# A sparse attention kernel: each query's first edge without TensorE, and gathers that skip empty places by a bound on the row number

## The chip, the cores and the metric

One core of one Trainium2 chip. The time is the device time of one launch in microseconds (us), the median of several executions. In the experiments the kernel before ran beside the others on the same chip; a ratio is the mean time of one kernel's fast runs over that of the kernel before in the same rounds, so it is not quite the ratio of the medians quoted.

Engine names in the profile: PE is TensorE, DVE is VectorE, ACT is ScalarE, POOL is GpSimd, SP is SyncE (it issues plain DMAs). "Granted clock" is the share of full speed that the throttle left to TensorE.

## The reference, cut to what matters

Graph attention on 16 batches of 1024 nodes, 512 wide, 8 heads, one adjacency matrix for all batches, then a residual and a normalisation:

```python
q = (x @ Wq + bq);  k = (x @ Wk + bk);  v = (x @ Wv + bv)       # heads of 64
scores = einsum('bqhd,bkhd->bhqk', q, k) / sqrt(64) + (1 - adj) * -1e9
out = einsum('bhqk,bkhd->bqhd', softmax(scores), v) @ Wo + bo
return layernorm(x + out)
```

The adjacency has 4043 edges of a million places, so the kernel works edge by edge. A query without an edge (60 of them) gets the mean of all rows of v; this is why a batch's gathers cannot start before its mean row exists. All four biases are zero in these inputs; one experiment uses that.

## The kernel before

A batch has eight tiles of 128 queries. A tile's edges are laid out in blocks of 128 places; a block is gathered as one row of q and one row of k|v for each place. VectorE makes the products and scores, ScalarE the exponentials, VectorE weighs v with them (`pv`), and TensorE adds the places of each query with a 0/1 matrix (`sums`). Then come the division, a transposition (`poT`), the product with Wo (`po`), the residual and the normalisation. GpSimd adds the output bias to a tile's residual rows `y` ahead of the residual, and raises the variance to the power -1/2 (`rstd`, the "root" of the prediction). y_1, y_5 are the second and the sixth of these additions at a change of batch, counted from y_0.

The order of instructions is fixed by one loop over blocks. In each step it issues a gather some blocks ahead, the VectorE work of the next blocks, the sum of this block, and then spends a credit of TensorE time on large products: `finishing` (po of tiles done) or, if there is none, `fronts` (q, k, v of the next batch).

```python
BLOCKS = (11, 6, 4, 4, 3, 3, 3, 3)           # blocks of the eight tiles: 37 per batch

def load_y(b, t):                            # the residual rows of a tile
    Y[b, t] = work.tile([P, D], F32, tag="y", bufs=7)
    nc.sync.dma_start(Y[b, t], x[b, ds(t * P, P), :])
    later(2, lambda: nc.gpsimd.tensor_tensor(Y[b, t], Y[b, t], bo_bc, op=OP.add))

def gather(n):
    ...
    nc.gpsimd.indirect_dma_start(out=QG[n], in_=q_rows[b % 2], ...)    # 128 rows of q
    nc.gpsimd.indirect_dma_start(out=KG[n], in_=kv_rows[b % 2], ...)   # 128 rows of k|v

def add_up(n):
    if i == 0:
        SUM[b, t] = psum.tile([P, 2, HALF], F32, tag="sum", bufs=2)
    nc.tensor.matmul(SUM[b, t][:, 0, 0:HD2], m, pv[:, 0:HD2], **kw)
    nc.tensor.matmul(SUM[b, t][:, 1, 0:HD2 + HEADS], m, pv[:, HD2:], **kw)

while ...:                                   # one step per block n
    if front_batches < B and front_batches <= max(n // NB, 0) + 1:
        fronts += ...                        # the next batch's products become available
    elif n % NB == 0:
        share = (sum(u[0] for u in fronts) + tiles * NPAIR * PRODUCT) / NB
    ... gather(gathered); weigh(n + 1); scores(n + 2)
    for fn in plan.pop(n, ()): fn()          # what `later` has put here
    ... exponentials(n + 2); add_up(n)
    for tile_done in done[:2]:
        if tile_done not in Y: load_y(*tile_done)
    ... spend the credit on finishing or fronts
```

## Time and profile before

| | before |
|---|---|
| time, median | 2593.45 us (2592.3 to 2593.49) |
| TensorE busy | 96% |
| granted clock, mean | 0.982 |
| period of one batch (mean of 13) | 153.7 us |
| TensorE idle at a change of batch | 1.9 us |

From the page of the kernel before, the 40 slices of TensorE, GpSimd and the granted clock (a digit is tenths busy, or tenths of full clock):

```profile
PE   6988999999999999999999999999999999999967
POOL 0156755647566574756647465564756557475675
PEclk9989999999999999999999999999999999999978
```

TensorE is full except at both ends. GpSimd looks half idle, which says nothing about whether it is late at one moment of each batch. Its gathers, as groups (busy us and mean ns of one, idle time before them and what ended most of it):

```profile
L506 POOL DMA_INDIRECT kvg<-kv_rows,key_row x592 | 588.7, 994 | 195.2 <-issue 182.9 <-DMA kv_rows<-mean 7.8 <-ACT pv L522 1.7
L501 POOL DMA_INDIRECT qg<-q_rows,query_row x592 | 586.9, 991 | 588.1 <-DVE s L517 453.7 <-issue 81.3 <-DVE stats L471 30.4
```

A pair of gathers costs GpSimd two microseconds, 592 times. And the waits of TensorE between 430 and 2420 us, that is without the two end batches (total, times, longest):

```profile
PE sum L545 <- DVE pv L533: 26.8, 15, 1.9
PE poT L566 <- DVE o L557: 1.8, 10, 0.2
```

### The profile page before, as it was taken

How to read it: one execution, taken by the hardware profiler on the slowest of the kernel's cores; microseconds unless marked ns; L12 is line 12 of the kernel's file. 1: busy time of each engine (PE TensorE's matmuls, PEld its weight loads, DVE VectorE, ACT ScalarE, POOL GpSimd, SP SyncE). 2: the span in 40 equal slices, each digit the busy share in tenths (PEclk: the TensorE clock that was granted, in tenths of full speed). 3: DMA queues.
4: the chain of work that ended last, by engine and by line, in shares of the span. 5: the costliest groups of instructions: out<-in, count | busy, mean ns of one | idle time of the engine just before them, and what ended most of it. 6: DMA issues, size and time to landing. Idle time of an engine off the chain costs nothing.

```text
span 2594.1 us, 26742 instructions
## 1 busy us (share of the span) xinstructions
PE 2477.6 (96%) x7659; PEld 1352.6 (52%) x7659; DVE 1968.2 (76%) x3613; ACT 698.7 (27%) x1764; POOL 1499.0 (58%) x1717
## 2 busy tenths in 40 slices
PE   6988999999999999999999999999999999999967
PEld 3545555555555555555555555555555555555534
DVE  5668778778778877877777777877877777787766
ACT  1345322222222222222222222222222222222254
POOL 0156755647566574756647465564756557475675
PEclk9989999999999999999999999999999999999978
DMA  4368887887879788787878878787887978878785
GB/s 154 110 243 290 270 291 247 286 270 271 283 237 307 254 291 267 257 292 244 301 253 292 271 235 306 244 294 256 277 288 233 309 251 287 264 256 287 230 277 179
DMA packets 228679, 678.01 MB, mean 261 GB/s; under 512 B 29454, under 2 KB 29466, under 8 KB 228524
## 3 DMA queue, kind: packets, MB, share of 16 engines
q0 software_dynamic: 132608, 465.64, 56.3%
q1 hardware_dynamic: 93344, 205.60, 21.2%
q10 hardware_dynamic: 2572, 4.99, 0.5%
q8 instruction: 62, 1.02, 0.2%
q14 instruction: 93, 0.76, 0.1%
HBM read 541.86 MB, written 134.25 MB: 261 GB/s over the span
## 4 chain that ended last, share of the span: by engine, by line
PE 68%; POOL 11%; DVE 10%; issue 7%; ACT 2%; DMA 1%; ACTq 0%; POOLq 0%; another core or an unknown queue 0%; SPq 0%; DVEq 0%
PE pv L377 16%; PE pk L377 15%; PE pq L377 15%; PE sum L546 7%; PE sum L545 7%; POOL kvg L506 4%; PE po L377 4%; POOL y L461 3%; POOL qg L501 2%; DVE y L468 2%; DVE stats L471 2%; PE pxT L359 2%; PE poT L566 2%; DVE qg L515 1%; DVE pv L533 1%
## 5 line engine op out<-in xcount | busy, mean ns | idle before, releaser
L501 POOL DMA_INDIRECT qg<-q_rows,query_row x592 | 586.9, 991 | 588.1 <-DVE s L517 453.7
L506 POOL DMA_INDIRECT kvg<-kv_rows,key_row x592 | 588.7, 994 | 195.2 <-issue 182.9
L533 DVE TENSOR_TENSOR pv<-kvg,pv 128x512 f32<-128x512 f32 x550 | 394.3, 717 | 223.1 <-ACT pv L522 146.8
L377 PE MATMUL pq<-wq,xT 128*128 128x512 f32 x1024 | 482.7, 597 | 14.7 <-ACT xT L363 13.2
L377 PE MATMUL pk<-wk,xT 128*128 128x512 f32 x1024 | 488.9, 598 | 7.1 <-ACT xT L363 7.1
L377 PE MATMUL pv<-wv,xT 128*128 128x512 f32 x1024 | 479.1, 593 | 0.0
L377 PE MATMUL po<-wo,oT 128*128 128x512 f32 x1024 | 473.9, 602 | 0.0
L515 DVE TENSOR_TENSOR qg<-qg,kvg 128x512 f32<-128x512 f32 x592 | 432.6, 731 | 0.3 <-issue 0.3
L517 DVE TENSOR_REDUCE s<-qg 128x8 f32<-128x512 f32 x592 | 406.1, 686 | 20.5
L545 PE MATMUL sum<-pv,sums 128*128 128x256 f32 x1184 | 361.6, 387 | 46.4 <-DVE pv L533 33.8
L545 PEld LDWEIGHTS sum<-pv,sums 128*128 128x128 f32 x1184 | 222.2, 192 | 326.5 <-issue 239.0
L522 ACT ACTIVATE pv<-s 128x8 f32<-128x8 f32 x592 | 124.1, 210 | 929.2 <-DVE s L517 626.5
L546 PE MATMUL sum<-pv,sums 128*128 128x264 f32 x1184 | 366.6, 392 | 4.6 <-ACT pv L529 2.3
L377 PEld LDWEIGHTS pk<-wk,xT 128*128 128x128 f32 x1024 | 194.3, 192 | 193.3 <-issue 175.7
L377 PEld LDWEIGHTS po<-wo,oT 128*128 128x128 f32 x1024 | 192.9, 194 | 182.6 <-issue 173.3
L377 PEld LDWEIGHTS pv<-wv,xT 128*128 128x128 f32 x1024 | 190.5, 191 | 167.0 <-issue 158.4
L377 PEld LDWEIGHTS pq<-wq,xT 128*128 128x128 f32 x1024 | 187.1, 192 | 159.2 <-issue 135.0
L546 PEld LDWEIGHTS sum<-pv,sums 128*128 128x128 f32 x1184 | 226.2, 192 | 41.6 <-ACT pv L529 6.4
L461 POOL TENSOR_TENSOR y<-y,bo_bc 128x512 f32<-128x512 f32 x128 | 163.4, 1277 | 141.5 <-ACT pv L522 74.7
L468 DVE TENSOR_TENSOR y<-po,y 128x512 f32<-128x512 f32 x128 | 88.0, 688 | 151.5 <-POOL y L461 139.4
L404 DVE TENSOR_TENSOR kv<-pk,bk_bc 128x512 f32<-128x512 f32 x128 | 88.2, 689 | 115.8 <-PE pk L377 87.2
L389 DVE TENSOR_REDUCE nrm<-sq 128x8 f32<-128x512 f32 x256 | 172.9, 676 | 1.4 <-ACT sq L388 1.4
(98 smaller groups left out, 1664.8 us busy)
## 6 DMA issues: line engine op xcount, KB each, us to landing
kv_rows<-kv SPq DMA_DIRECT2D x128, 512.0 KB
x<-in_x_dram SPq DMA_DIRECT2D x128, 256.0 KB
q_rows<-q SPq DMA_DIRECT2D x128, 256.0 KB
y<-in_x_dram SPq DMA_DIRECT2D x128, 256.0 KB
out_dram<-y SPq DMA_DIRECT2D x128, 256.0 KB
qg<-q_rows,query_row POOLq DMA_INDIRECT x592
kvg<-kv_rows,key_row POOLq DMA_INDIRECT x592
a<-in_adj_dram SPq DMA_DIRECT2D x8, 512.0 KB
```

Of the source, the lines that this page charges most:

```text
L377: nc.tensor.matmul(p, lhs()[:, ts(c, P)], w[:, c, :], start=(c == 0), stop=(c == NPAIR - 1))
L389: later(1, lambda: nc.vector.tensor_reduce(NRM[b][:, i, t, :], sq.rearrange("p (h d) -> p h d", d=HD), axis=AX.X, op=OP.add))
L461: later(2, lambda: nc.gpsimd.tensor_tensor(Y[b, t], Y[b, t], bo_bc, op=OP.add))
L468: nc.vector.tensor_tensor(y, p, y, op=OP.add)
L501: nc.gpsimd.indirect_dma_start(out=QG[n], out_offset=None, in_=q_rows[b % 2], in_offset=bass.IndirectOffsetOnAxis(ap=query_row[:, g:g + 1] ...
L506: nc.gpsimd.indirect_dma_start(out=KG[n], out_offset=None, in_=kv_rows[b % 2], in_offset=bass.IndirectOffsetOnAxis(ap=key_row[:, g:g + 1], ...
L515: nc.vector.tensor_tensor(m, m, KG[n][:, 0:D], op=OP.mult)
L517: nc.vector.tensor_reduce(S[n], m.rearrange("p (h d) -> p h d", d=HD), axis=AX.X, op=OP.add)
L522: nc.scalar.activation(PV[n][:, D:], S.pop(n), AF.Exp)
L533: nc.vector.tensor_tensor(pv[:, 0:D].rearrange("p (h d) -> p h d", d=HD), v[:, D:].rearrange("p (h d) -> p h d", d=HD), pv[:, D:, None].to ...
L545: nc.tensor.matmul(SUM[b, t][:, 0, 0:HD2], m, pv[:, 0:HD2], **kw)
L546: nc.tensor.matmul(SUM[b, t][:, 1, 0:HD2 + HEADS], m, pv[:, HD2:], **kw)
```

## The change

Intent: the first edge of each query goes into one extra block per tile in which place p belongs to query p. Such a block needs no 0/1 matrix: its q rows are a plain load, and its `pv` is added by VectorE to what TensorE has summed. 29 blocks per batch remain on TensorE, and 8 go past it. And a place without an edge gets a row number above a bound, so that its row is not fetched. The core of the diff:

```diff
-BLOCKS = (11, 6, 4, 4, 3, 3, 3, 3)
+BLOCKS = (10, 5, 3, 3, 2, 2, 2, 2)
+NO_ROW = 65536.0
...
-            return psum.tile([P, HALF], F32, tag="fill", name=name, bufs=4)
+            return psum.tile([P, HALF], F32, tag="fill", name=name, bufs=6)
...  (lists of rows: a place without an edge becomes NO_ROW)
-                nc.vector.tensor_scalar(e[:, 1, :], e[:, 1, :], -1.0, 0.0, op0=OP.add, op1=OP.max)
-                nc.vector.tensor_scalar(key_row[:, g0:g0 + n], e[:, 1, :], float(N), None, op0=OP.min)
-                nc.vector.tensor_copy(query_row[:, g0:g0 + n], g[:, :, J + 1])
+                nc.vector.tensor_scalar(e[:, 1, :], e[:, 1, :], -1.0, None, op0=OP.add)
+                nc.vector.tensor_scalar(e[:, 0, :], e[:, 1, :], 0.0, NO_ROW, op0=OP.is_lt, op1=OP.mult)
+                nc.vector.tensor_tensor(key_row[:, g0:g0 + n], e[:, 1, :], e[:, 0, :], op=OP.max)
+                nc.vector.tensor_tensor(query_row[:, g0:g0 + n], g[:, :, J + 1], e[:, 0, :], op=OP.max)
...  (gather)
+            if i == BLOCKS[t]:
+                nc.sync.dma_start(QG[n], q_rows[b % 2][ds(t * P, P), :])
+            else:
                 nc.gpsimd.indirect_dma_start(out=QG[n], ...,
+                    bounds_check=N - 1, oob_is_err=False)
             nc.gpsimd.indirect_dma_start(out=KG[n], ...,
+                bounds_check=N, oob_is_err=False)
...  (add_up and normalise)
-                SUM[b, t] = psum.tile([P, 2, HALF], F32, tag="sum", bufs=2)
+                PSUM[b, t] = psum.tile([P, 2, HALF], F32, tag="sum", bufs=1)
-            nc.vector.tensor_scalar(r, s[:, 1, HD2:HD2 + HEADS], 1.0e-30, None, op0=OP.max)
-            nc.vector.reciprocal(r, r)
-            ... two products of 256 columns with r
+            nc.vector.tensor_tensor(r, s[:, 1, HD2:HD2 + HEADS], pv[:, D:], op=OP.add)
+            nc.vector.tensor_tensor(o, s, pv[:, 0:D], op=OP.add)        # empties the accumulator
+            nc.vector.reciprocal(r, r)
+            nc.vector.tensor_tensor(o8, o8, r[...], op=OP.mult)
```

(The last lines are shortened; `o` and `s` are views.) Not shown: the loop now counts the sum of a block as 0.87 us of TensorE's time and takes it from the credit, and a tile is closed in the step of its extra block. So the order of TensorE's products at a change of batch moves too.

More of the change, by code (lines that the diff above doesn't have):

```diff
@@ L30 @@
 PRODUCT = 0.86
+SUM = 0.87
 TRANSPOSE = 0.44
@@ L173 @@
     assert N == 1024 and D == 512 and HD == 64
-    NB = sum(BLOCKS)
+    NS = sum(BLOCKS)
+    NB = NS + NT
     first = [sum(BLOCKS[:t]) for t in range(NT)]
@@ L224 @@
         nc.vector.tensor_scalar(bq_bc, bq_bc, scale, None, op0=OP.mult)
-        sums = one.tile([P, NB, P], F32, name="sums")
+        sums = one.tile([P, NS, P], F32, name="sums")
         key_row = one.tile([P, NB], I32, name="key_row")
-        query_row = one.tile([P, NB], I32, name="query_row")
+        query_row = one.tile([P, NS], I32, name="query_row")
         check = one.tile([P, 2 * NT], F32, name="check")
@@ L277, in edges @@
             st = small.tile([P, 4], F32, name="est")
-            deg, end, lim, lone = (st[:, i:i + 1] for i in range(4))
+            deg, end, lim, off = (st[:, i:i + 1] for i in range(4))
             kl = small.tile([P, J + 2], F32, tag=f"kl{J}", name=f"kl_{t}", bufs=2)
@@ L291, in edges @@
                     yield
-            nc.vector.tensor_scalar(lone, kl[:, 0:1], 0.0, N + 1.0, op0=OP.is_le, op1=OP.mult)
-            nc.vector.tensor_tensor(kl[:, 0:1], kl[:, 0:1], lone, op=OP.add)
-            nc.vector.tensor_scalar(deg, deg, 1.0, None, op0=OP.max)
+            nc.vector.tensor_scalar(off, kl[:, 0:1], 0.0, N + 1.0, op0=OP.is_le, op1=OP.mult)
+            nc.vector.tensor_tensor(kl[:, 0:1], kl[:, 0:1], off, op=OP.add)
+            nc.vector.tensor_scalar(off, kl[:, 0:1], -1.0, 0.0, op0=OP.add, op1=OP.max)
+            nc.vector.tensor_scalar(key_row[:, NS + t:NS + t + 1], off, float(N), None, op0=OP.min)
+            nc.vector.tensor_scalar(deg, deg, -1.0, 0.0, op0=OP.add, op1=OP.max)
             yield
@@ L299, in edges @@
             yield
-            nc.vector.tensor_copy(kl[:, J:J + 1], po[:, 0:1])
+            nc.vector.tensor_copy(off, po[:, 0:1])
+            nc.vector.tensor_scalar(kl[:, J:J + 1], po[:, 0:1], -1.0, None, op0=OP.add)
             nc.vector.tensor_copy(kl[:, J + 1:J + 2], query[:, t:t + 1])
-            nc.vector.tensor_tensor(end, kl[:, J:J + 1], deg, op=OP.add)
+            nc.vector.tensor_tensor(end, off, deg, op=OP.add)
             nc.vector.tensor_scalar(lim, end, -float(nb * P), 0.0, op0=OP.add, op1=OP.max)
             nc.vector.scalar_tensor_tensor(
-                check[:, NT + t:NT + t + 1], deg, -float(J), lim, op0=OP.add, op1=OP.max
+                check[:, NT + t:NT + t + 1], deg, 1.0 - J, lim, op0=OP.add, op1=OP.max
             )
@@ L309, in edges @@
             o, span = of[:, 0:nb * P], place[:, 0:nb * P]
-            nc.vector.tensor_scalar(o, span, kl[:, J:J + 1], None, op0=OP.is_gt)
+            nc.vector.tensor_scalar(o, span, off, None, op0=OP.is_gt)
             nc.vector.scalar_tensor_tensor(o, span, end, o, op0=OP.is_le, op1=OP.mult)
@@ L490, in finish @@
             return product(f"po_{b}_{t}", lambda: OT[b, t], W["o"], out)
-        KG, QG, PV, SUM = {}, {}, {}, {}
-        blocks = [(b, t, i) for b in range(B) for t in range(NT) for i in range(BLOCKS[t])]
+        KG, QG, PV, PSUM = {}, {}, {}, {}
+        blocks = [(b, t, i) for b in range(B) for t in range(NT) for i in range(BLOCKS[t] + 1)]
         def gather(n):
             b, t, i = blocks[n]
-            g = first[t] + i
             QG[n] = work.tile([P, D], F32, tag="qg", name=f"qg_{n}", bufs=7)
-            nc.gpsimd.indirect_dma_start(
-                out=QG[n], out_offset=None, in_=q_rows[b % 2],
-                in_offset=bass.IndirectOffsetOnAxis(ap=query_row[:, g:g + 1], axis=0),
-            )
+            if i == BLOCKS[t]:
+                g = NS + t
+                nc.sync.dma_start(QG[n], q_rows[b % 2][ds(t * P, P), :])
+            else:
+                g = first[t] + i
+                nc.gpsimd.indirect_dma_start(
+                    out=QG[n], out_offset=None, in_=q_rows[b % 2],
+                    in_offset=bass.IndirectOffsetOnAxis(ap=query_row[:, g:g + 1], axis=0),
+                    bounds_check=N - 1, oob_is_err=False,
+                )
             KG[n] = work.tile([P, 2 * D], F32, tag="kvg", name=f"kvg_{n}", bufs=8)
@@ L508, in gather @@
                 in_offset=bass.IndirectOffsetOnAxis(ap=key_row[:, g:g + 1], axis=0),
+                bounds_check=N, oob_is_err=False,
             )
@@ L519, in exponentials @@
         def exponentials(n):
-            PV[n] = work.tile([P, D + HEADS], F32, tag="pv", name=f"pv_{n}", bufs=4)
+            b, t, i = blocks[n]
+            if i == BLOCKS[t]:
+                PV[n] = work.tile([P, D + HEADS], F32, tag="pv0", name=f"pv_{n}", bufs=2)
+            else:
+                PV[n] = work.tile([P, D + HEADS], F32, tag="pv", name=f"pv_{n}", bufs=4)
             nc.scalar.activation(PV[n][:, D:], S.pop(n), AF.Exp)
@@ L541, in add_up, with normalise @@
             if i == 0:
-                SUM[b, t] = psum.tile([P, 2, HALF], F32, tag="sum", name=f"sum_{b}_{t}", bufs=2)
+                PSUM[b, t] = psum.tile([P, 2, HALF], F32, tag="sum", name=f"sum_{b}_{t}", bufs=1)
             m, pv = sums[:, first[t] + i, :], PV.pop(n)
             kw = dict(start=(i == 0), stop=(i == BLOCKS[t] - 1))
-            nc.tensor.matmul(SUM[b, t][:, 0, 0:HD2], m, pv[:, 0:HD2], **kw)
-            nc.tensor.matmul(SUM[b, t][:, 1, 0:HD2 + HEADS], m, pv[:, HD2:], **kw)
-            if i == BLOCKS[t] - 1:
-                later(1, lambda: normalise(b, t))
-        def normalise(b, t):
-            s = SUM.pop((b, t))
-            r = small.tile([P, HEADS], F32, tag="rden", name=f"rden_{b}_{t}", bufs=2)
-            nc.vector.tensor_scalar(r, s[:, 1, HD2:HD2 + HEADS], 1.0e-30, None, op0=OP.max)
-            nc.vector.reciprocal(r, r)
-            o = work.tile([P, D], F32, tag="o", name=f"o_{b}_{t}", bufs=2)
-            for i in range(2):
-                nc.vector.tensor_tensor(
-                    o[:, ts(i, HD2)].rearrange("p (h d) -> p h d", d=HD),
-                    s[:, i, 0:HD2].rearrange("p (h d) -> p h d", d=HD),
-                    r[:, ds(i * HEADS // 2, HEADS // 2), None].to_broadcast([P, HEADS // 2, HD]), op=OP.mult,
-                )
+            nc.tensor.matmul(PSUM[b, t][:, 0, 0:HD2], m, pv[:, 0:HD2], **kw)
+            nc.tensor.matmul(PSUM[b, t][:, 1, 0:HD2 + HEADS], m, pv[:, HD2:], **kw)
+        def normalise(n):
+            b, t, i = blocks[n]
+            s, pv = PSUM.pop((b, t)), PV.pop(n)
+            o = work.tile([P, D], F32, tag="o", name=f"o_{b}_{t}", bufs=2)
+            r = small.tile([P, HEADS], F32, tag="rden", name=f"rden_{b}_{t}", bufs=2)
+            nc.vector.tensor_tensor(r, s[:, 1, HD2:HD2 + HEADS], pv[:, D:], op=OP.add)
+            nc.vector.tensor_tensor(
+                o.rearrange("p (a d) -> p a d", a=2), s[:, :, 0:HD2], pv[:, 0:D].rearrange("p (a d) -> p a d", a=2),
+                op=OP.add,
+            )
+            nc.vector.reciprocal(r, r)
+            o8 = o.rearrange("p (h d) -> p h d", d=HD)
+            nc.vector.tensor_tensor(o8, o8, r[:, :, None].to_broadcast([P, HEADS, HD]), op=OP.mult)
             def transpose():
@@ L578 @@
         done = []
+        for i in range(8):
+            nc.gpsimd.memset(work.tile([P, 2 * D], F32, tag="kvg", name=f"kvg_first_{i}", bufs=8), 0.0)
+        for i in range(7):
+            nc.gpsimd.memset(work.tile([P, D], F32, tag="qg", name=f"qg_first_{i}", bufs=7), 0.0)
         total = len(blocks)
@@ L603 @@
                     tiles = len(done) + (NT if n + NB < total else NT + 2)
-                    share = (sum(u[0] for u in fronts) + tiles * NPAIR * PRODUCT) / NB
+                    share = (sum(u[0] for u in fronts) + tiles * NPAIR * PRODUCT + NS * SUM) / NB
                 while gathered < min(n + AHEAD + 1, total) and blocks[gathered][0] in set_up:
@@ L611 @@
                     scores(n + 2)
+                if 0 <= n < total and blocks[n][2] == BLOCKS[blocks[n][1]]:
+                    normalise(n)
                 for fn in plan.pop(n, ()):
@@ L615 @@
                     exponentials(n + 2)
-                if 0 <= n < total:
+                credit += share
+                if 0 <= n < total and blocks[n][2] < BLOCKS[blocks[n][1]]:
                     add_up(n)
+                    credit -= SUM
                 for tile_done in done[:2]:
@@ L620 @@
                         load_y(*tile_done)
-                credit += share
                 first_unit = True
```

## The prediction

> **What bounds the kernel now.** I read the page first (busy times, the 40 slices), then TensorE's timeline with every wait ahead of an instruction, then the timelines of GpSimd and VectorE in the stretch where those waits fall, and last the order of instructions of both kernels.
>
> From the page, then TensorE's timeline at some batch boundaries (start us, duration us, instruction, in brackets the idle time before it and who ended it):
>
> ```profile
> PE 2477.6 (96%) x7659; PEld 1352.6 (52%) x7659; DVE 1968.2 (76%) x3613; ACT 698.7 (27%) x1764; POOL 1499.0 (58%) x1717
> ...
> 469.02 0.70 PE L545 MATMUL sum<-pv,sums 128*128 128x256 f32 x2 [1.88 <-DVE pv L533]
> 622.33 0.70 PE L545 MATMUL sum<-pv,sums 128*128 128x256 f32 x2 [1.88 <-DVE pv L533]
> 775.83 0.70 PE L545 MATMUL sum<-pv,sums 128*128 128x256 f32 x2 [1.89 <-DVE pv L533]
> 1082.85 0.70 PE L545 MATMUL sum<-pv,sums 128*128 128x256 f32 x2 [1.88 <-DVE pv L533]
> 1085.03 0.68 PE L566 MATMUL poT<-ident,o 128*128 128x128 f32 x4 [0.18 <-DVE o L557]
> ```
>
> TensorE runs without a gap through a batch of about 153.5 us (622.33 - 469.02 = 153.3; twelve periods up to the one at 2315.14 give a mean of 153.84) and stops once, at the change of batch, for 1.88 + 0.18 = 2.06 us. So the time is nearly TensorE's work, and one wait per batch. What sits behind that wait (GpSimd, then VectorE, same boundary; the product for the mean row, from which the next batch's gathers may start, began on TensorE at 1043.62):
>
> ```profile
> 1043.62 1.02 PE L428 MATMUL pm<-vsum,mean 128*1 128x512 f32 x2
> ...
> 1045.97 1.02 POOL L501 DMA_INDIRECT qg<-q_rows,query_row  x1 [0.76 <-DMA kv_rows<-mean]
> 1053.26 1.27 POOL L461 TENSOR_TENSOR y<-y,bo_bc 128x512 f32<-128x512 f32 x1
> 1058.87 1.27 POOL L461 TENSOR_TENSOR y<-y,bo_bc 128x512 f32<-128x512 f32 x1
> 1064.59 1.28 POOL L461 TENSOR_TENSOR y<-y,bo_bc 128x512 f32<-128x512 f32 x1
> 1069.97 1.27 POOL L461 TENSOR_TENSOR y<-y,bo_bc 128x512 f32<-128x512 f32 x1
> 1079.06 1.27 POOL L461 TENSOR_TENSOR y<-y,bo_bc 128x512 f32<-128x512 f32 x1
> ...
> 1052.74 2.36 DVE L533 TENSOR_TENSOR pv<-kvg,pv 128x512 f32<-128x512 f32 x1
> 1080.37 0.69 DVE L468 TENSOR_TENSOR y<-po,y 128x512 f32<-128x512 f32 x1 [5.34 <-POOL y L461]
> 1082.11 0.68 DVE L533 TENSOR_TENSOR pv<-kvg,pv 128x512 f32<-128x512 f32 x1
> ```
>
> From 1045.97 to 1080 GpSimd has no pause but its issue gaps: a pair of gathers, an addition y, a square root, again and again, 5.4 to 5.7 us per round, while TensorE and VectorE want a round in about 4. VectorE is held 5.34 us for the y at 1079.06, and only behind it in its queue stands the product pv that TensorE waits for. So **the batch change is a race of two chains from the mean row: TensorE's list of products, and GpSimd's list**. Today they arrive nearly together.
>
> **What the Trainium skill says.** "Perfetto Trace Analysis", Identifying the Most-Contended Engine: matmul busy time is a poor measure of distance from roofline, and the same gap repeating on the engine that should be saturated points at a missing buffer. The trace agrees with half: the same 1.88 us gap does repeat, but behind it is a slow engine, not a buffer. "TensorE: Matmul & The Clock Gate", Part 1: after an idle window of about 3.4 us the array runs at half clock until about 3.4 us of work have passed. The trace agrees: the one boundary with a long wait (5.58 us, at 301.88) shows
>
> ```profile
> 298.00:300.00 2.00, 0.00 (x0) 0.50 0.66 254
> 302.00:304.00 2.00, 2.00 (x6) 0.50 0.74 111
> 308.00:310.00 2.00, 2.00 (x9) 1.00 0.81 279
> ```
>
> (stretch, length, TensorE busy, granted clock, DMA share, GB/s), while the waits of 1.88 us leave it at 1.00. "SBUF — State Buffer", Who interferes with whom: a VectorE instruction with two SBUF inputs and a GpSimd one that reads SBUF exclude each other. The trace agrees: the pv at 1052.74 took 2.36 us instead of 0.68, over the y of 1053.26. "DMA: Bandwidth & Descriptors", Issuing engines are not separate DMA queues: another issuing engine saves only issue time. No page has the cost of a bounds check in a gather.
>
> **The change part by part.**
> (1) Each query's first edge leaves TensorE. Blocks that multiply on TensorE go from 37 to 29 per batch, 8 x 16 = 128 fewer in all. One is two halves of 0.43 and 0.45 us from start to start (1038.34, 1038.77, 1039.21), so 7.04 us per batch, 112.6 us in all, 4.3%. It is on the path wherever TensorE sets the pace.
> (2) The number of gather blocks stays 37; 8 of the query gathers per batch become plain loads from the SP queue. GpSimd saves 8 x (0.95 + 0.30 gap) = 10 us per batch. But none of these lies in the round of the batch change: the gathers issued there belong to the next batch's first tile, whose ten blocks are all query gathers.
> (3) Skipped rows: of 3712 places per batch in the indirect blocks 3079 hold an edge (counted from the inputs), so 633 rows of 6 KB are not moved, 62 of 678 MB. The waits show no transfer that holds VectorE back, so this is worth nothing. In the first tile 1276 of 1280 places are full.
> (4) VectorE's closing of a tile becomes one small addition, one 128x512 addition, a reciprocal and one 128x512 product, for one small maximum, a reciprocal and two 128x256 products: +0.6 us x 128 = 80 us, 1968 to about 2050. In mid-batch VectorE delivers pv 6 to 8 us before TensorE takes it (ends of L533 against starts of L545), so this stays hidden there.
> (5) The accumulator in PSUM goes from two buffers to one. A tile's first sum now waits until VectorE has added the previous tile out of PSUM, which stands 2.9 us behind the pv it waited for before: hidden by the 6 to 8 us in mid-batch, not at the batch change.
> (6) **The order at the batch change.** Before, from the mean product, TensorE had 25 units of `po`, then 8 blocks, and seven units of the next batch (6 us) ahead of the sum that had to wait. In the changed order nothing of the next batch stands ahead: it runs the mean product 0.95, 22 units of po (0.86 each), 4 blocks (0.88) and 2 transposes (0.44), 24.3 us, and comes directly to the first sum of the new batch. In VectorE's order that sum's pv now stands behind y_5, and the accumulator's release (scores, sum, addition) behind that.
> GpSimd's list from the same product to y_5, with this trace's durations: start +2.35 (1045.97 - 1043.62), three pairs 7.29, two rounds 5.61 + 5.72, the last y, root, pair, root, pair 9.09, y_5 itself 1.27: 31.3 us. One round fewer than before, because y_1 now comes ahead of the gathers. Then VectorE: y and statistics 1.74, pv 0.60, score product 0.71, reduction 0.61, the small addition 0.19, the addition out of PSUM 0.70: 4.6 us. The sum can start at 35.9; TensorE is there at 24.3. **Wait 11.6 us instead of 2.06.**
> (7) 11.6 us idle halves the clock. What that cost in the four long waits of the first batch: at 155.90 6.4 us for 3.9 of work, at 178.30 3.6 for 2.1, at 222.80 3.3 for 1.7, at 301.88 6.8 for 3.9; mean 2.1 us.
> Sum per batch: -7.04 + (11.6 - 2.06) + 2.1 = +4.6 us. Fourteen boundaries of this kind: +65 us. The last batch is bound by GpSimd and should lose some 8 of its 10 us; the first (waits on the adjacency loads) some 2. 2593 + 65 - 10 = 2648 us.
>
> **The rivals.**
> (A) TensorE's work is what counts, and the boundary wait stays as it is: 2593 - 113 = 2480, faster by 4%. For it: 96% busy, gaps of 2 us. Against it: the two lists above; GpSimd's gets only one round shorter, TensorE's 13 us.
> (B) As I say, but without the clock loss or with GpSimd's rounds shorter by a third, since VectorE collides less: wait 7 to 9 us, 2560 to 2620, within 2%.
> (C) The bounds check makes a gather slower on GpSimd. Fourteen gathers lie in the list; each 0.1 us adds 1.4 us per batch, 20 us in all: 2670 and more. Nothing in this trace says how much.
> (D) VectorE becomes the bound in mid-batch: about 126 us of work in a batch of 144. It had waits on TensorE's key and query products there, so I expect it to keep up.
>
> **Range and chances.** The chain's durations are measured and the order is fixed, so the wait is good to 2 us either way, 28 us over 14 boundaries; the clock loss to 0.7 (10 us), the check and the two end batches to some 30. Range 2595 to 2700. The 2% line above lies at 2645, almost at my value: slower 0.52, within 2% 0.40. For faster the wait would have to stay below 5 us, which would need an error in the lists: 0.08.
>
> **What would show it right or wrong.** Right: one wait of 9 to 14 us per batch ahead of the first sum of a batch, released by VectorE's addition of the tile's close; VectorE's y before it waiting on GpSimd; granted clock 0.50 after it; TensorE's busy time down by about 80 us or more, its idle up; a period near 158 us. Wrong: a period near 146 us with waits under 3 us (rival A), gathers on GpSimd well off 0.95 us (C), or waits spread over all tiles (the single accumulator or VectorE, D).

One reference in it needs mending: that a repeating gap can mean a missing buffer stands in the Trainium skill's "Perfetto Trace Analysis" under Optimization Strategy, just behind the section that the prediction names, and there as a possibility only. What it says of issuing engines no run here tests by itself. And one reading of its trace fails: the waits of 1.88 us did not leave the clock at 1.00 everywhere (see point 7 below).

## The result, and the profile after

| | before | after |
|---|---|---|
| time, median | 2593.47 us | 2675.43 us (2671.13 to 2678.53) |
| ratio | 1 | 1.0312 (95% interval 1.0294 to 1.0331) |
| TensorE busy | 96% | 89% |
| granted clock, mean | 0.982 | 0.947 |
| period of one batch (mean of 13) | 153.7 us | 159.1 us |
| moved by DMA | 678.0 MB | 615.9 MB |

Slower by 3.1%, although TensorE has 536 products less. The page after: busy times, then the slices of TensorE and of the clock, then the two groups of gathers.

```profile
PE 2383.3 (89%) x7123; PEld 1273.2 (48%) x7123; DVE 2033.4 (76%) x3646; ACT 695.6 (26%) x1764; POOL 1470.5 (55%) x1604
...
PE   7979798998989989798997989899898998989865
PEclk9989899998989989898998989999898998989988
...
L517 POOL DMA_INDIRECT qg<-q_rows,query_row x464 | 488.6, 1053 | 680.2 <-DVE s L535 479.6
L523 POOL DMA_INDIRECT kvg<-kv_rows,key_row x592 | 634.2, 1071 | 227.4 <-issue 172.1
```

TensorE's row, all 9 before, now has dents, about one per batch, and the clock has them as well. A gather is 0.06 to 0.08 us longer than before. The waits of TensorE in the same stretch without the end batches:

```profile
PE sum L567 <- DVE rden L580: 170.7, 13, 15.6
```

13 waits hold it all: one per batch, 13.1 us on the mean. TensorE's timeline at one of them (the columns as in the prediction), from the product of the mean row:

```profile
909.31 1.02 PE L439 MATMUL pm<-vsum,mean 128*1 128x512 f32 x2
...
933.19 0.61 PE L568 MATMUL sum<-pv,sums 128*128 128x264 f32 x2
947.69 1.19 PE L567 MATMUL sum<-pv,sums 128*128 128x256 f32 x2 [13.89 <-DVE rden L580]
```

and what GpSimd and VectorE did meanwhile:

```profile
909.93 1.26 POOL L472 TENSOR_TENSOR y<-y,bo_bc 128x512 f32<-128x512 f32 x1
...
913.07 1.08 POOL L517 DMA_INDIRECT qg<-q_rows,query_row  x1 [0.61 <-issue]
...
921.24 1.27 POOL L472 TENSOR_TENSOR y<-y,bo_bc 128x512 f32<-128x512 f32 x1
926.57 1.28 POOL L472 TENSOR_TENSOR y<-y,bo_bc 128x512 f32<-128x512 f32 x1
932.38 1.28 POOL L472 TENSOR_TENSOR y<-y,bo_bc 128x512 f32<-128x512 f32 x1
...
941.83 1.27 POOL L472 TENSOR_TENSOR y<-y,bo_bc 128x512 f32<-128x512 f32 x1
```
```profile
943.13 0.69 DVE L479 TENSOR_TENSOR y<-po,y 128x512 f32<-128x512 f32 x1 [5.70 <-POOL y L472]
...
944.87 0.68 DVE L555 TENSOR_TENSOR pv<-kvg,pv 128x512 f32<-128x512 f32 x1
...
946.87 0.68 DVE L576 TENSOR_TENSOR o<-sum,pv 128x512 f32<-128x512 f32 x1
```

TensorE has done its list at 933.80 (the start of its next sum at 947.69 less the wait of 13.89), 24.5 us behind the mean product. GpSimd reaches the last addition y at 941.83, VectorE waits 5.70 us for it, and only then come `pv` of the new batch's first block and, two microseconds behind it, the addition `o` that empties the single accumulator. The first sum starts at 947.69, when that is over (947.55). This is the picture of the prediction. The clock behind the wait (stretch, length, TensorE busy, granted clock, DMA share, GB/s):

```profile
942.00:946.00 4.00, 0.00 (x0) 0.50 0.64 243
946.00:950.00 4.00, 2.31 (x5) 0.50 0.68 211
950.00:954.00 4.00, 4.00 (x10) 0.69 0.70 212
954.00:958.00 4.00, 4.00 (x11) 1.00 0.92 305
```

Where the time came from, by the start of each batch's mean product in the two profiled runs (2594.1 and 2675.5 us long): up to the third batch +2.9 us (430.04 to 432.93), thirteen periods of +5.38 us (69.9), and from the last mean product to the end +8.6 us (165.6 to 174.1; this holds the fourteenth change of batch as well). Together 81.4 us.

### The profile page after: what moved, and what is told of

Its sections match the earlier page's. It is cut to its first block, busy times and chain, and to the rows that moved or that the text cites. A ratio compares the mean times of both kernels' runs of the same rounds, so it can differ in the third digit from the quotient of the medians.

```text
span 2675.5 us, 26519 instructions
## 1 busy us (share of the span) xinstructions
PE 2383.3 (89%) x7123; PEld 1273.2 (48%) x7123; DVE 2033.4 (76%) x3646; ACT 695.6 (26%) x1764; POOL 1470.5 (55%) x1604
## 4 chain that ended last, share of the span: by engine, by line
PE 59%; DVE 13%; POOL 11%; issue 11%; DMA 4%; ACT 1%; another core or an unknown queue 0%; POOLq 0%; SPq 0%; ACTq 0%; DVEq 0%
PE pq L388 15%; PE pk L388 14%; PE pv L388 13%; PE sum L567 6%; PE sum L568 5%; POOL kvg L523 5%; PE po L388 3%; POOL qg L517 3%; POOL y L472 3%; DVE stats L482 2%; DVE y L479 2%; DVE qg L533 2%; PE pxT L370 2%; DVE s L535 2%; DVE pv L555 2%
## 5 line engine op out<-in xcount | busy, mean ns | idle before, releaser
L517 POOL DMA_INDIRECT qg<-q_rows,query_row x464 | 488.6, 1053 | 680.2 <-DVE s L535 479.6
L523 POOL DMA_INDIRECT kvg<-kv_rows,key_row x592 | 634.2, 1071 | 227.4 <-issue 172.1
L567 PE MATMUL sum<-pv,sums 128*128 128x256 f32 x928 | 294.6, 401 | 247.9 <-DVE rden L580 225.6
L388 PE MATMUL pq<-wq,xT 128*128 128x512 f32 x1024 | 495.9, 615 | 13.0 <-ACT xT L374 13.0
L388 PE MATMUL pk<-wk,xT 128*128 128x512 f32 x1024 | 475.6, 593 | 0.0
L388 PE MATMUL po<-wo,oT 128*128 128x512 f32 x1024 | 460.6, 596 | 0.0
L533 DVE TENSOR_TENSOR qg<-qg,kvg 128x512 f32<-128x512 f32 x592 | 417.2, 705 | 0.0
L567 PEld LDWEIGHTS sum<-pv,sums 128*128 128x128 f32 x928 | 177.4, 198 | 458.5 <-issue 402.8
L568 PE MATMUL sum<-pv,sums 128*128 128x264 f32 x928 | 296.8, 403 | 1.3 <-ACT pv L551 0.8
L388 PEld LDWEIGHTS pq<-wq,xT 128*128 128x128 f32 x1024 | 194.1, 199 | 172.5 <-issue 150.8
L479 DVE TENSOR_TENSOR y<-po,y 128x512 f32<-128x512 f32 x128 | 87.9, 687 | 151.5 <-POOL y L472 144.6
L568 PEld LDWEIGHTS sum<-pv,sums 128*128 128x128 f32 x928 | 183.6, 199 | 32.5 <-ACT pv L551 4.5
```

Source lines behind the costliest of these rows:

```text
L388: nc.tensor.matmul(p, lhs()[:, ts(c, P)], w[:, c, :], start=(c == 0), stop=(c == NPAIR - 1))
L479: nc.vector.tensor_tensor(y, p, y, op=OP.add)
L517: nc.gpsimd.indirect_dma_start(out=QG[n], out_offset=None, in_=q_rows[b % 2], in_offset=bass.IndirectOffsetOnAxis(ap=query_row[:, g:g + 1] ...
L523: nc.gpsimd.indirect_dma_start(out=KG[n], out_offset=None, in_=kv_rows[b % 2], in_offset=bass.IndirectOffsetOnAxis(ap=key_row[:, g:g + 1], ...
L533: nc.vector.tensor_tensor(m, m, KG[n][:, 0:D], op=OP.mult)
L567: nc.tensor.matmul(PSUM[b, t][:, 0, 0:HD2], m, pv[:, 0:HD2], **kw)
```

## The experiments

The theory: at each change of batch the end of GpSimd's list (gathers of the new batch, with the additions y between them) sets the first sum, and TensorE, which is done 13 us earlier, has nothing else to do. The rivals: the single accumulator; the bounds check in the gathers; VectorE. Twelve kernels ran, all with correct results. "Mean product" below is the zero point of each batch change. Positions and waits are means over the changes between the first and the last batch, the gathers' and y's also with the last one.

| run | time, us | ratio to before | wait per batch, us | period, us |
|---|---|---|---|---|
| before | 2593 to 2595 | 1 | 1.9 | 153.7 |
| after | 2675.4 | 1.0312 | 13.1 | 159.1 |
| two_sums | 2648.8 | 1.0194 | 11.4 | 157.3 |
| no_bound | 2675.2 | 1.0300 | 13.5 | 159.6 |
| check_no_skip | 2696.8 | 1.0386 | 14.2 | 160.7 |
| bound_only (of before) | 2606.4 | 1.0039 | 2.2 | 154.6 |
| no_y_add | 2522.5 | 0.9715 | 4.3 | 150.2 |
| warm | 2664.4 | 1.0278 | 2.8 | 158.2 |
| y_early | 2475.1 | 0.9532 | 1.6 | 145.4 |
| shift | 2464.2 | 0.9492 | mostly none | 144.6 |
| shift_y | 2445.6 | 0.9426 | none | 143.7 |
| before_shift_y (of before) | 2545.9 | 0.9813 | none | 150.4 |
| shift_y_two | 2445.4 | 0.9428 | none | 143.6 |
| shift_y_nob | 2437.4 | 0.9390 | none | 143.4 |

### Two accumulators again

```diff
-            return psum.tile([P, HALF], F32, tag="fill", name=name, bufs=6)
+            return psum.tile([P, HALF], F32, tag="fill", name=name, bufs=4)
-                PSUM[b, t] = psum.tile([P, 2, HALF], F32, tag="sum", ..., bufs=1)
+                PSUM[b, t] = psum.tile([P, 2, HALF], F32, tag="sum", ..., bufs=2)
```

> The changed kernel (2675 us), with two accumulators for the sums in PSUM again, as before, instead of one. My theory, the two lists at the batch change: the first sum of a batch then waits for its own product pv alone, not for the addition that empties the accumulator, which stands about 2.9 us behind it; the wait of about 13 us becomes 10 to 10.5, still released by VectorE behind the y that GpSimd adds, and each later batch is 2.5 to 3 us shorter, 35 to 45 us in all; the last batch, whose sums waited on the accumulator at five tiles, gets shorter too, by 3 to 8. Time 2625 to 2640. Rival, the single accumulator is the cause: the wait goes back to about 2 us and the time to about 2500. Rival, VectorE as a whole is the bound: nothing moves, 2665 to 2680.

Measured 2648.75 us (ratio 1.0194, interval 1.0168 to 1.0219). TensorE's wait and VectorE's work ahead of it:

```profile
945.15 1.19 PE L567 MATMUL sum<-pv,sums 128*128 128x256 f32 x2 [12.21 <-DVE pv L555]
```
```profile
942.57 0.69 DVE L479 TENSOR_TENSOR y<-po,y 128x512 f32<-128x512 f32 x1 [5.70 <-POOL y L472]
...
944.32 0.68 DVE L555 TENSOR_TENSOR pv<-kvg,pv 128x512 f32<-128x512 f32 x1
```

The releaser has changed from the accumulator's to `pv` itself, and VectorE waits 5.70 us for GpSimd as before. So the single accumulator is 1.8 us of the wait and 27 us of the 82; it is not the cause of the rest. The gain was less than I expected (2625 to 2640, and 2.9 us per batch change; from the mean product to the first sum it was 1.7 us, 37.7 to 36.0). The edit also takes two of the six buffers of the large products away; this run alone cannot tell what that costs.

### The products kept warm

```diff
+                if n > 0 and n % NB == NB - 1:                 # end of a batch
+                    idle = fill_psum(f"idle_{n}")
+                    for _ in range(12):
+                        nc.tensor.matmul(idle, W["q"][:, 0, 0:P], W["q"][:, 1, :], start=True, stop=True)
```

> The changed kernel with twelve products of no use (about 10 us) on TensorE ahead of the first sum of each new batch, in the time in which it waits. If the low clock after the wait costs time, as my prediction has it with 2.1 us per batch, the granted clock stays at 1.00 behind the wait and the time falls by 20 to 32 us, to 2643 to 2655. If the cost of the clock is hidden (VectorE or GpSimd set the pace just behind the wait as well), the time stays within 5 us of 2675. If the dummies come too long, it rises.

Measured 2664.44 us: 11 us, half of what I expected. The trace shows why. The end of the wait and what follows it, in two batches of this kernel (columns as above):

```profile
621.00:623.00 2.00, 0.03 (x1) 1.00 0.37 129
623.00:625.00 2.00, 2.00 (x9) 1.00 0.78 197
...
777.00:779.00 2.00, 0.00 (x0) 1.00 0.47 119
779.00:781.00 2.00, 1.69 (x4) 0.54 0.74 168
781.00:783.00 2.00, 2.00 (x6) 0.60 0.71 268
```

Behind the dummies a wait of 2 to 4 us was left, and the clock fell behind it in 9 of 13 batches. From the first sum of a batch to the second block's sum TensorE takes 8.26 us in the four batches that stayed warm, 10.54 us on the mean after the change without dummies, and 9.58 us on the mean with them. So the low clock costs 2.3 us per batch, which confirms the term of the prediction (2.1), and this kernel regained 1.0 of it. That fits its period, 0.9 us shorter.

### Without GpSimd's addition

```diff
-            later(2, lambda: nc.gpsimd.tensor_tensor(Y[b, t], Y[b, t], bo_bc, op=OP.add))
```

> The changed kernel without GpSimd's addition of the output bias to y (the bias is zero in these inputs, so the result stays right). My theory says that GpSimd's list sets the batch change: four to five such additions of 1.27 us stand in it ahead of the product that the first sum waits for, so the wait falls from 13 to 7 to 8 us, the clock stays higher, and the time falls by 70 to 90 us, to 2585 to 2605. Rival, VectorE or the single accumulator alone sets the wait: under 15 us of gain. Rival, gathers wait for the transfer of the new batch's rows and not for GpSimd's time: under 15 us.

Measured 2522.49 us (0.9715): 153 us off the changed kernel, twice what I expected, and faster than the kernel before. TensorE, then VectorE ahead of the first sum:

```profile
896.42 0.61 PE L567 MATMUL sum<-pv,sums 128*128 128x264 f32 x2
901.29 1.19 PE L566 MATMUL sum<-pv,sums 128*128 128x256 f32 x2 [4.26 <-DVE rden L579]
```
```profile
896.60 0.68 DVE L478 TENSOR_TENSOR y<-po,y 128x512 f32<-128x512 f32 x1
...
898.47 0.68 DVE L554 TENSOR_TENSOR pv<-kvg,pv 128x512 f32<-128x512 f32 x1
...
900.47 0.68 DVE L575 TENSOR_TENSOR o<-sum,pv 128x512 f32<-128x512 f32 x1
```

No bracket in front of VectorE's instructions: it waits for nobody now. I had taken four additions of 1.27 us off GpSimd's list. But without the addition VectorE's y needs nothing from GpSimd, so the whole list leaves the chain: the first sum comes 28.8 us behind the mean product instead of 37.7, and what is left, a wait of 4.3 us, is VectorE's own list. This shows that GpSimd's additions were the link, and it shows the next limit behind it.

### The bounds check, and the bytes that it saves

Four kernels belong together: with check and skipping (the change), with neither, with the check alone, and the kernel before with both.

```diff
  no_bound: row numbers clamped as before the change, no clearing of the gathers' buffers at the start, and
-                    bounds_check=N - 1, oob_is_err=False,      # both gathers
  check_no_skip: row numbers clamped as before the change, both bounds_check left in
```

> The changed kernel without the bounds check: a place without an edge fetches a row again (row 0 or the zero row), as before the change, and all rows are moved. If the check makes a gather slower on GpSimd by the 0.06 to 0.09 us that the page shows (1.05 and 1.07 us against 0.99), 14 gathers in the list at the batch change are worth 0.8 to 1.3 us, 11 to 19 us in all: 2655 to 2665, with the wait ahead of the first sum down from 13 to about 12. If the check is the main cause of the loss, the time falls below 2600. If skipping rows is worth something (62 MB less to move), the kernel gets slower than 2675.

> The changed kernel (2675 us) with the bounds check left on every gather, but with no place to skip: a place without an edge fetches a row again, so all bytes are moved. It parts the two effects that seemed to cancel in the run without the check. If they do cancel (the check costs GpSimd 1.3 us over the list at the batch change; the bytes saved let the load of the first residual rows land 1.5 us earlier, which lets the gathers start earlier), this kernel has the first loss without the gain: the gathers start 4.4 us behind the mean product instead of 2.8, the wait goes from 13.0 to 14 to 14.8, and the time is 2690 to 2705. If the bytes saved are worth nothing, as my prediction had it, the time stays within 5 us of 2675. If skipped places were what makes a gather slower, the gathers take 1.00 us here and the time is below 2665.

> The kernel before (2594 us) with the bounds check and the skipped places alone; every block still goes through TensorE. The run without the check showed two things that cancel: a gather costs GpSimd 0.06 us more with it, 1.3 us over the list at the batch change, but with less to move the load of the residual rows y that GpSimd waits for lands 1.5 us earlier. If both hold here as well, the wait of 2 us at the batch change hardly moves and the time is 2588 to 2606. If the check's cost stands alone, the wait grows to 3.3 us and the time is 2610 to 2620. If the bytes saved win, it falls below 2585.

Without the check nothing came of it: 2675.23 us for 2675.43, outside the expected 2655 to 2665, though the gathers were back at 1.00 us on the mean. The positions behind the mean product, in us:

| | first y of GpSimd | first gather | last y of GpSimd | first gather to last y | period |
|---|---|---|---|---|---|
| after | -3.20 | 2.79 | 31.79 | 29.00 | 159.11 |
| no_bound | -1.54 | 4.61 | 32.30 | 27.69 | 159.58 |
| check_no_skip | -1.68 | 4.42 | 33.24 | 28.82 | 160.66 |

The check makes GpSimd's list 1.1 us longer (27.69 to 28.82, both with all bytes moved). Skipping lets the list begin 1.6 us earlier (4.42 to 2.79, both with the check). The two nearly cancel. The gain of the skipping is all in this earlier start (from the first gather to the last y it is 29.00 with skipping, 28.82 without). Its link is the load of the residual rows for GpSimd's first y. In the changed kernel the profile names this load in 14 of GpSimd's waits ahead of a y (total, times, longest), and puts others down to "issue" or to ScalarE:

```profile
POOL y L472 <- DMA y<-in_x_dram: 38.1, 14, 7.8
```

Here it is with the full bytes, in check_no_skip: the load's issue, the addition that stood behind it, and the stretches before that (stretch, length, granted clock, share of the 16 DMA engines, GB/s).

```profile
906.92 0.42 SPq L470 DMA_DIRECT2D y<-in_x_dram  x1
```
```profile
916.02 1.68 POOL L471 TENSOR_TENSOR y<-y,bo_bc 128x512 f32<-128x512 f32 x1 [6.96 <-issue]
```
```profile
913.00:915.00 2.00, 1.00 1.03 397
915.00:917.00 2.00, 1.00 0.86 334
917.00:919.00 2.00, 1.00 0.11 43
```

The addition starts 9.1 us after the load's issue, when the DMA engines have fallen nearly idle. In the changed kernel at the change shown above the issue was at 899.66, the addition began at 907.16, 7.5 us later, and the DMA engines fell idle about a microsecond sooner after the issue:

```profile
905.00:907.00 2.00, 1.00 1.03 381
907.00:909.00 2.00, 1.00 0.66 257
909.00:911.00 2.00, 1.00 0.02 8
```

Over all 14 changes the load is issued 9.57 us ahead of the mean product in each of the three kernels, and the addition starts 6.4 us behind the issue with skipping, 7.9 and 8.0 us without (in the kernel before 6.3, with check and skipping 4.6). The landing itself is not in the trace; that it sets the addition is concluded from this.

In time: the check costs 21.6 us (2696.8 for 2675.2; 22 by the ratios; 2.9 of it lie ahead of the third batch, where the buffers are cleared as well) and the skipped rows bring 21.4 us (2696.8 for 2675.4; 19 by the ratios). The expectation of check_no_skip, 2690 to 2705, held. In the kernel before, check and skipping together cost 10 to 13 us (by the ratio and by the medians): the first y is 1.7 us earlier there too (-2.68 for -0.99), but the gathers start only 0.35 us earlier, so the cost is the larger part. The time of 2606.44 us lies 0.4 above the expected range. The wait grew from 1.9 to 2.2 us:

```profile
621.91 0.70 PE L550 MATMUL sum<-pv,sums 128*128 128x256 f32 x2 [2.22 <-DVE pv L538]
```

### The residual rows early

```diff
-                for tile_done in done[:2]:
-                    if tile_done not in Y:
-                        load_y(*tile_done)
+                yb, yt = divmod(next_y, NT)
+                if yb < B and n >= yb * NB + 8 + 2 * yt and next_y - len(out_done) < 7:
+                    load_y(yb, yt)
+                    next_y += 1
...
-                    if not fronts and not finishing and done and n > loaded.get(done[0], n):
+                    if not fronts and not finishing and done and n > loaded.get(done[0], n) + 1:
```

> The changed kernel with the residual rows y of a tile loaded, and the bias added by GpSimd, in the middle of the batch instead of at its end; the additions are all still done, but none stands between the gathers of the next batch's first tile. My theory (the position of this work on GpSimd costs the time, not its amount): close to the run without the addition, wait ahead of the first sum 4 to 6 us, now with VectorE's own list as what is waited for, time 2520 to 2550. If the amount of GpSimd's work counts, or the extra reads of y collide with VectorE in mid-batch, it stays above 2600.

Measured 2475.14 us (0.9532), 45 us below the range's lower end. All additions are still there (GpSimd is even busier, 62% for 55%), but in mid-batch. So the position costs, not the amount. That it beats the kernel without any addition has a second reason which I had not planned: with y always loaded, the loop also lets the last po products of a batch run sooner, and VectorE's first y behind the mean product starts 0.2 us behind it for 3.1 us there. The wait is 1.57 us, and the clock stays at 1.00 behind it in all 13 changes between the first and the last batch (the first sum takes 0.67 us, not 1.19):

```profile
890.19 0.67 PE L568 MATMUL sum<-pv,sums 128*128 128x256 f32 x2 [1.58 <-DVE rden L581]
```

### The next batch's products early

```diff
+SHIFT = 4
-                if front_batches < B and front_batches <= max(n // NB, 0) + 1:
+                if front_batches < B and front_batches <= max((n + SHIFT) // NB, 0) + 1:
-                elif n % NB == 0:
-                    tiles = len(done) + (NT if n + NB < total else NT + 2)
+                elif n == 0 or (n + SHIFT) % NB == 0:
+                    tiles = NT if n + NB < total else len(done) + NT + 2
```

> The changed kernel with TensorE's next work moved: the products of the following batch begin four steps before the end of a batch, so that some of them stand ahead of the first sum of the new batch; GpSimd's and VectorE's lists stay as they are. If the loss is TensorE standing idle behind a list that it could have filled, the wait of 13 us shrinks to 0 to 5, the clock stays at 1.00, and the time is 2490 to 2545. If GpSimd's list is the bound of the whole batch (no slack elsewhere in it), the wait moves to another place and the time stays above 2620.

> The two repairs at once: early y, and the next batch's products four steps early. Both lists at the batch change then have slack: no wait over 2 us from batch 2 on, granted clock at 0.98 or above, and the time is TensorE's work: 2594 less 112 for the blocks, less some 25 for the waits of 2 us that go as well, plus up to 10 for the last batch: 2455 to 2500. If VectorE bounds mid-batch (its work is about 127 us of a period of 146), waits on it appear inside the batches and the time stays above 2510.

Shift alone gave 2464.17 us (0.9492), with early y 2445.61 us (0.9426, interval 0.9411 to 0.9442); both beat both kernels, and both were faster than I expected. With shift alone GpSimd's and VectorE's lists are as late as ever; TensorE only has other work in the meantime. This is the Trainium skill's advice in "Perfetto Trace Analysis", Optimization Strategy: where the most-contended engine changes over time, interleave the regimes. The trace agrees: between 290 and 2270 us the waits of TensorE are 8.5 us in all with shift, and with both repairs

```profile
PE sum L569 <- DVE rden L582: 1.2, 3, 0.4
PE poT L589 <- DVE o L584: 0.3, 1, 0.3
```

against 170.7 us in the changed kernel. VectorE, busy 85% of the time, does not hold TensorE anywhere in mid-batch.

### The same repairs on the kernel before, and two more

```diff
  before_shift_y: the two repairs above, applied to the kernel before
  shift_y_two:    shift_y with two accumulators (as in two_sums)
  shift_y_nob:    shift_y without the bounds check (as in no_bound)
```

> The kernel before, with both repairs (early y, the next batch's products four steps early) and without the change. If the change is worth what its removed blocks take on TensorE once nothing waits at the batch change, this kernel only loses the waits of 2.06 us (14 times 2.06, 29 us) and lies at 2550 to 2575, so that the repaired change (2446) is 105 to 125 us below it, for 128 blocks of 0.88 us. If the gain is the repairs' own, this kernel falls below 2500 too.

> The repaired changed kernel (both repairs, 2446 us) with two accumulators for the sums again. In its trace the only waits on the accumulator's release are in the last batch (five of 2.4 to 4.9 us), so if they end the time there, this gives 5 to 12 us, 2434 to 2441. If the last batch is bound by GpSimd and VectorE behind it, nothing comes of it, 2442 to 2449; if the smaller number of PSUM buffers for the products (four instead of six) matters, it is slower than 2449.

> The repaired changed kernel without the bounds check, so every place fetches a row (62 MB more). With slack on GpSimd and in the transfers at the batch change, neither the check's 0.06 us per gather nor the bytes saved should show: 2440 to 2452. If the check slows GpSimd where it counts, this kernel is below 2438; if the saved bytes count, it is above 2454.

The kernel before gains from the repairs too, to 2545.89 us (0.9813), 4 us below my range and far above 2500. So with both repaired the change is worth 100 us, 4%. The periods say it more cleanly: 150.43 us repaired before, 143.46 us repaired after (the typical period of shift_y_nob), a difference of 6.97 us, which is the 7.04 us of eight blocks. The page of the repaired kernel before, to be set beside 2344.9 us of TensorE busy in shift_y:

```profile
PE 2460.4 (97%) x7659; PEld 1351.3 (53%) x7659; DVE 1993.4 (78%) x3613; ACT 691.1 (27%) x1764; POOL 1559.0 (61%) x1717
```

Two accumulators gave nothing more (2445.44), the second outcome that I had named: the waits on the accumulator in the last batch gave way to waits on `pv`, which ScalarE makes there for most blocks. Dropping the bounds check gave 8 us more (2437.40, interval 0.9373 to 0.9407, just clear of shift_y's). I had thought "no effect", 2440 to 2452, likelier; this lies just inside the other outcome, a check that still counts. Of 6.3 us between the two profiled runs 4.9 are in the last batch and 3.3 in the fourteen periods, while the start lost 1.9. This is the fastest kernel, 6% below the one before: the first half of the change with another order of work, and without its second half. Set beside before_shift_y, which has no check either, it is 108.5 us faster, within the 105 to 125 that I had named for the blocks.

## Why the prediction was right

It named 2648 us and the step by which a change that takes work off the full engine makes the kernel slower; measured were 2675. Point by point:

1. Eight blocks less on TensorE, 7.04 us per batch: right. The repaired pair shows 6.97.
2. The saved query gathers do not lie in the batch change: right; GpSimd's list there is first gathers and y, as written.
3. "Worth nothing" for the skipped rows: **wrong**. They bring 21 us, through an earlier landing of a load that I had not counted as waiting for bytes. Rival C, the check's cost of 20 us per 0.1 us of a gather, was right in kind; by that rule the 0.06 us that a gather grew by give 12 us, and the check cost 21.6. Both effects were left out of the sum, and that did no harm because they have the same size: luck, not insight.
4. VectorE hidden in mid-batch: right. No wait on it there in any kernel, even at 85% busy; the few short ones lie within 32 us behind a mean product. Its own time grew by 65 us (1968 to 2033), for 80. Rival D falls.
5. The single accumulator counts only at the batch change, and in the last batch: right in place. Its size there was 1.7 us, not 2.9: the 2.9 were counted from the start of `pv`, whose own time TensorE has to wait for in either case.
6. The race of the two lists: right. TensorE's list took 24.5 us for 24.3. GpSimd's last y was to start at 30.0 us (31.3 less its own 1.27) and started at 31.8: gathers began at 2.79 on the mean instead of 2.35 (2.58 on the mean in the kernel before), and the check made the list 1.1 us longer. Two y stand ahead of the gathers, as predicted; where the second begins behind the mean product, the gathers begin at 3.8, elsewhere at 2.1 to 3.4. VectorE's part was right to 0.1 us (from the last y to the first sum 5.9). So the wait was 13.1 us, not 11.6.
7. The low clock, 2.1 us per batch: measured 2.3. But that the kernel before pays none of it is **wrong**: in 3 of its 13 changes the clock fell to 0.50 behind a wait of 1.9 us, and from the first sum to the second block's TensorE took 5.68 us for 4.42. One of them (TensorE, then the stretch as above):

```profile
1389.43 1.00 PE L545 MATMUL sum<-pv,sums 128*128 128x256 f32 x2 [1.89 <-DVE pv L533]
```
```profile
1390.00:1392.00 2.00, 2.00 (x6) 0.50 0.61 170
```

Summed per batch the prediction had +4.6, the traces have +5.38. The terms as measured, -6.97 + (13.1 - 2.2) + 2.3 = +6.2 (2.2 is all that TensorE waited per batch before, 28.6 us in 13), overshoot that by 0.9 us. The repaired kernel before explains the direction: its period is 3.4 us shorter than before's (150.36 for 153.73), of which the waits are 2.2, so the old batch change cost 1.2 us more than its waits. The three lowered clocks are 0.3 of that on the mean of the batches. The rest is work that takes longer: outside the waits TensorE took 151.2 us for a batch that kept its clock, 150.4 in the repaired kernel; why is not shown.

The prediction is 27 us below the measured time. Of these 12 lie behind the last mean product: the prediction has one more change there (+4.6) and -8 us for the last batch, and it took +8.6. Only 2 of the 12 are the wait there (it grew by 11.4, 1.5 to 12.9, for 9.5); the other 10 are blocks and gathers that brought less than I gave them. TensorE is busy 124 of the last 166 us before the change, so blocks taken from it bring little, while the sums wait for the one accumulator at five tiles (9.45 us the longest). I had credited GpSimd's saved gathers there without asking what the sums wait for. 5 lie ahead of the third batch (+2.9 for -2), and 10 in the thirteen periods (69.9 for 60). The chances (0.52 for slower by more than 2%, 0.40 for within 2%) had left it nearly open whether the loss would pass 2%.

Rival A (2480 us, faster by 4%) was wrong for this kernel as it stands, and right as a statement of what the change is worth once the batch change is repaired.

## What to carry to other kernels

When an engine is 96% busy and you take work off it, look for the one place per iteration where it meets the other engines, and count each engine's list from a common event to that place: the engine that you unload will only arrive earlier at the same appointment. If another engine's list is longer there, the cheap repair is order, not speed: move that engine's side work away from the place, or give the waiting engine work of the next iteration. A saving and a cost that come in one edit can cancel, so try them apart before you call either of them nothing.

## What the Trainium skill lacked or had wrong

- No page has the cost of a bounds check in an indirect gather. Here a gather of 128 rows took GpSimd 1.05 to 1.07 us with it and 0.99 to 1.01 us without, skipped rows or not, and a stretch of GpSimd's work with 14 of them became 1.1 us longer (27.69 to 28.82).
- "Perfetto Trace Analysis", Optimization Strategy, reads the same gap repeating on the engine that should be saturated as a possible lack of buffers. Here a second buffer took 1.8 us from a gap of 13.1 us; the rest was the order of work on another engine. The same section's advice to interleave regimes was the right one: 2675 to 2464 us.
- "TensorE: Matmul & The Clock Gate", Part 1, gives about 3.4 us of idle time to the drop of the clock. Here waits of 2.19 to 2.34 us behind a full stretch were followed by a lowered clock in some batches and not in others (granted 0.54 behind a wait of 2.34 us, 1.00 behind one of 2.29 us), so the length of the wait alone does not decide it. In the kernel before, 3 of 13 waits of 1.88 to 1.90 us were followed by 0.50. The page's remark that the window runs freely would allow this; its number cannot be used as a safe limit.
- No page has how long a load of 256 KB takes to land among other transfers. Here the work that needed it began 7.9 us behind its issue with all rows moved and 6.4 us with 62 MB (9%) less, at a mean use of the DMA engines of 75% and 71% of the span; this set the change of batch and was worth 21 us.
